# First convolution on TensorE in two row groups, start-up loads moved between queues, the last softmax inverse formed on VectorE, and a new order of both ends

## The chip, the cores and the metric

The kernel runs on one core of a Trainium2 chip. The core has TensorE (matrix products), VectorE, ScalarE and GpSimd (elementwise work), and SyncE, which here only issues transfers (DMA). The metric is device time in microseconds (us), lower is better. Names in profile rows: PE is TensorE, PEld its weight loads, DVE is VectorE, ACT is ScalarE, POOL is GpSimd, SP is SyncE; SPq and ACTq are the queues in which SyncE and ScalarE issue transfers.

## What is computed

The input is x of shape 4 x 128 x 64 x 64 (batch, channels, rows, columns). Layer 0 is a normalisation over channels, a depthwise 3x3 convolution with its input added, and attention of every pixel over its 5x5 neighbourhood inside a 16x16 window, in two branches of four heads. Layer 1 is a causal linear attention over the 4096 pixels of an image in order, then a recurrence over the pixels. Cut to what matters:

```python
y = layernorm2d(x, ln_g, ln_b)
y = y + cpe(y)                       # depthwise 3x3, edges repeated
q, k, v = Wq @ y, Wk @ y, Wv @ y     # per 16x16 window, branch and head
logits = q . patches(k) * scale      # 5x5 neighbours, zero outside the window
o = softmax(logits) . patches(v)
x = x + (Wo @ o, both branches) / rect
t = tokens(x)                        # 4 x 4096 x 128
t = t + num / den                    # elu features, cumulative sums of k v and of k
wx = batchnorm(layernorm(t) @ W.T)   # mean and variance over all tokens
y_t = sigmoid(wx_t + y_(t-1) @ V.T)  # along the 4096 tokens
out = t + y
```

A neighbour outside the window has a zero key, so it counts with a logit of 0: the denominator of the softmax is the sum over the neighbours inside plus the number of those outside, a constant of the pixel.

## The kernel before

**Tiling.** The image of a batch is cut into four bands of 16 rows (1,024 pixels), 16 bands in all, and a band into four windows of 16x16, 64 in all. Tiles have 128 channels or 128 pixels on the partitions.

**Steps of a band.** `norm_rows(n)` normalises the rows: `measured` takes statistics on VectorE (`bn_stats`, `bn_aggr`) and forms the inverse deviation on GpSimd with a power (L294, L295); `normed` scales on VectorE (L302); `turned` transposes on TensorE (L311); ScalarE evicts into `ypad`, a tile of 18 x 66 with its edges, which GpSimd fills by copies (L369 to L377). Then `taps` does the depthwise convolution: the first tap on ScalarE (L385), the other eight on VectorE (L387). The centre weight has 1 added, so that the input comes in with it (L820, on VectorE). For band 0 alone, two of four windows take another way, `multiply_first`: nine matmuls with diagonal matrices that ScalarE has made from the identity (L822), in two steps of four and five taps (L405). Windows 0 and 1 go through `convolve_first`, that is, `taps`.

**Steps of a window.** q, k (L436) and v (L449) are products with an eviction by ScalarE; v is moved between partition halves by two transfers (L458, L459). `logits` opens four PSUM banks with a mask product (L476), adds the products of q and k (L489), and ScalarE takes the exponentials (L498). `weighted` has three steps: sums (L518, with a copy `den` and a transfer that gathers it into a compact 128x32 tile `dc`, L526), values (L533, copy `o_sb` L541), and inverse: VectorE adds the count of outside neighbours (L544) and takes the reciprocal (L546), one transfer writes it to DRAM (`rd`, L550), another spreads it over all partitions (`rden`, L552). `scaled` multiplies `o_sb` by `rden` on GpSimd (L561) into `oT`, one tile for a band. `in_range` checks every four windows that the denominators are in range (L507, L508).

**Layer 1** works by half bands ("a" and "c"; in the end, "y" and "z" are those of the band before, "v" and "w" of the one before that): output projection and residual (L587, L594), measure, norm, turn, keys and queries (L634 to L638), values (L650), turn_keys (L663), scores (L671, L673), accumulate (L688, L696), attend (L707 to L721), keep (L726), measure_last, send and spread (per-token factors through DRAM, L618 and L629), and product (L748 to L755), which leaves the inputs of the recurrence. The last half, c of band 15, is normalised on the spot instead (norm_last, turn_last, L739 to L745).

**The recurrence** (L1026, L1031) runs over all segments at once after a global batch statistic (L741), with GpSimd adding and SyncE writing the output. It isn't touched.

**What sets the order.** Three lists of words. `START` is the order in which the first four windows are begun, with "front" as one step of the generator that prepares the following bands, and "warm.n" as n extra matmuls on zeros (`fill`, L268) before the next bank. `SLOT` with `AHEAD` and `LAYER1` is the order inside every later window. `TAIL` is the order of what remains after the logits of window 63. `in_order` (L912) then fixes that order on TensorE, VectorE, ScalarE and GpSimd; SyncE's queue isn't fixed by it. A weight tile comes in by `loaded`, on SyncE's or on ScalarE's queue:

```python
    load(0, 2)
    load_head(1)
    ln_g = loaded("ln_g", [P, 1], eng=nc.scalar)
    ln_b = loaded("ln_b", [P, 1], eng=nc.scalar)
    cpe_w = loaded("cpe_w", [P, 9], eng=nc.scalar)
    cpe_b = loaded("cpe_b", [P, 1], eng=nc.scalar)
    wqT = loaded("wqT", [P, BR * P], eng=nc.scalar)
```

## Time and profile before

| | us |
|---|---|
| median of 3 runs | 827.42 (825.77 to 827.80) |
| the profiled execution | 831.01 |
| its span | 829.3 |
| TensorE busy | 800.6 |
| VectorE busy | 689.7 |
| first q product starts (L436) | 19.37 |
| sums of window 3 (L518) start | 52.26 |
| first output projection (L587) starts | 67.31 |
| last logits (L489) end | 719.70 |
| output projection of the last band, half a (L587), starts | 734.40 |
| statistics of the last half (L740) end | 769.87 |

The times of the middle rows are from the start of the span, by the timeline and the chain of waits. The profile is of one execution; its own time is a little above the median of the others, so sums are made against it. In a row of the profile's groups the text reads: line, engine, operation, output <- input, partitions x elements, count, busy time, mean duration in ns of one, then the engine's idle time just before it and what ended that. A matmul with fp32 operands takes two passes, so TensorE shows twice the count of the source. A row of busy time by stretches reads: the stretch, its length, busy time (and count) of PE, PEld, DVE, ACT and POOL, the granted clock of TensorE as a share of full speed, the mean busy share of the 16 DMA engines, and GB/s.

### The profile page before, as it was taken

What the parts mean: (1) busy time and instruction counts of PE and PEld (TensorE: products, weight loads), DVE (VectorE), ACT (ScalarE), POOL (GpSimd) and SP (SyncE); (2) the same over time, 40 slices, a digit from 0 to 9 for tenths busy, and PEclk for the clock granted to TensorE, in tenths of its full rate; (3) what the DMA queues carried; (4) which work ended last, traced back from release to release, by engine and by line L of the source; (5) the groups of instructions that cost most, each with busy time, mean ns of one, the idle gap of its engine ahead of it and who ended that gap; (6) DMA issues with size and microseconds to landing.
All of it is one profiled execution on the core that took longest, in us unless ns stands there. A gap on an engine that the chain in (4) does not pass through costs nothing.

```text
span 829.3 us, 28925 instructions
## 1 busy us (share of the span) xinstructions
PE 800.6 (97%) x11811; PEld 642.3 (77%) x11817; DVE 689.7 (83%) x2134; ACT 530.6 (64%) x1022; POOL 254.9 (31%) x365
## 2 busy tenths in 40 slices
PE   7998999999999999999999999999999999988894
PEld 4776887878787878778787878788787878776693
DVE  6655989998989988998989898898989897378885
ACT  3775767676757576666767675766667675723683
POOL 2133241423233232413242322323231422231094
PEclk9998999999999999999999999999999999999997
DMA  5122141422323231414133232313141212211797
GB/s 142 21 64 71 43 120 39 88 75 69 85 70 96 62 100 33 114 42 112 48 84 77 63 93 70 96 39 108 43 120 41 80 53 69 69 53 39 240 206 206
DMA packets 81566, 69.33 MB, mean 84 GB/s; under 512 B 44816, under 2 KB 63888, under 8 KB 81424
## 3 DMA queue, kind: packets, MB, share of 16 engines
q1 hardware_dynamic: 53344, 44.00, 18.5%
q10 hardware_dynamic: 27072, 19.72, 8.8%
q0 software_dynamic: 1008, 3.67, 2.5%
q8 instruction: 95, 1.56, 0.9%
q14 instruction: 47, 0.39, 0.2%
HBM read 40.03 MB, written 17.89 MB: 70 GB/s over the span
## 4 chain that ended last, share of the span: by engine, by line
PE 89%; DVE 4%; DMA 3%; POOL 2%; issue 1%; ACT 0%; ACTq 0%; POOLq 0%; SPq 0%; DVEq 0%
PE bank L436 13%; PE bank L489 8%; PE bank L518 7%; PE bank L587 7%; PE bank L533 7%; PE bank L449 6%; PE bank L634 6%; PE bank L311 6%; PE z L1026 4%; PE bank L671 3%; PE bank L650 3%; PE bank L707 3%; PE bank L688 3%; PE bank L709 3%; PE bank L748 3%; PE bank L476 3%
## 5 line engine op out<-in xcount | busy, mean ns | idle before, releaser
L387 DVE SCALAR_TENSOR_TENSOR y<-ypad,cpe_w,y 128x512 f32<-128x512 f32 x240 | 184.2, 767 | 16.5 <-ACT y L385 12.0
L498 ACT ACTIVATE es<-bank 128x512 f32<-128x512 f32 x256 | 132.2, 602 | 32.4 <-PE bank L489 32.4
L294 POOL TENSOR_SCALAR rs<-mv 128x4 f32<-128x4 f32 (+2 forms) x100 | 25.5, 255 | 377.8 <-DVE mv L292 373.1
L561 POOL TENSOR_TENSOR oT<-o_sb,rden 128x512 f32<-128x512 f32 x64 | 83.4, 1304 | 122.1 <-DMA rden<-rd 87.4
L295 POOL TENSOR_TENSOR rs<-rs,mhalf 128x4 f32<-128x4 f32 (+2 forms) x100 | 106.0, 1060 | 8.3
L533 PEld LDWEIGHTS bank<-es,v_sb 128*32 128x32 f32 x3072 | 62.7, 110 | 37.0 <-issue 32.0
L444 ACT COPY k<-bank 128x512 f32<-128x512 f32 x64 | 38.6, 604 | 66.2 <-PE bank L436 66.2
L489 PE MATMUL bank<-q,k 32*64 32x160 f32 (+1 forms) x4096 | 77.6, 274 | 0.0
L489 PEld LDWEIGHTS bank<-q,k 32*64 32x64 f32 x4096 | 75.3, 130 | 2.7
L587 PEld LDWEIGHTS bank<-woT,oT 128*128 128x128 f32 x512 | 62.3, 199 | 12.7 <-POOL oT L561 8.9
L518 PE MATMUL bank<-es,ones 128*32 128x512 f32 x512 | 68.4, 605 | 0.1
L533 PE MATMUL bank<-es,v_sb 128*32 128x96 f32 (+1 forms) x3072 | 68.5, 237 | 0.0
L587 PE MATMUL bank<-woT,oT 128*128 128x128 f32 x512 | 63.2, 283 | 4.8 <-POOL oT L561 4.8
L436 PE MATMUL bank<-y2w,wqT 128*128 128x256 f32 x256 | 66.5, 382 | 0.7 <-DVE y2w L387 0.6
L521 ACT COPY den<-bank 128x512 f32<-128x512 f32 x64 | 37.4, 584 | 45.1 <-PE bank L518 45.0
L436 PE MATMUL bank<-y2w,wkT 128*128 128x256 f32 x256 | 66.0, 380 | 0.0
L449 PE MATMUL bank<-wvT,y2w 128*128 128x256 f32 x256 | 65.7, 379 | 0.0
L634 PE MATMUL bank<-xl,awT 128*128 128x512 f32 x128 | 63.1, 594 | 1.0 <-ACT xl L611 1.0
L636 ACT ACTIVATE low<-bank,minus 128x512 f32<-128x512 f32 x64 | 44.0, 687 | 21.9 <-PE bank L634 20.2
L544 DVE TENSOR_TENSOR dc<-dc,pad_c 128x32 f32<-128x32 f32 x64 | 23.7, 371 | 41.0 <-DMA dc<-den 40.8
L444 ACT COPY q<-bank 128x512 f32<-128x512 f32 x64 | 38.7, 605 | 27.6 <-PE bank L436 21.5
L290 DVE BATCH_NORM_STATS2 st<-x 128x6 f32<-128x128 f32 x256 | 55.3, 278 | 0.5
(137 smaller groups left out, 1685.8 us busy)
## 6 DMA issues: line engine op xcount, KB each, us to landing
rden<-rd SPq DMA_DIRECT2D x64, 256.0 KB
v_sb<-v_sb SPq DMA_DIRECT2D x128, 64.0 KB
factors<-factors ACTq DMA_DIRECT2D x31, 256.0 KB
xin<-in_xt SPq DMA_DIRECT2D x15, 512.0 KB
out<-rs_o ACTq DMA_DIRECT2D x16, 256.0 KB
resd<-rs_o ACTq DMA_DIRECT2D x16, 256.0 KB
out<-ot SPq DMA_DIRECT2D x32, 128.0 KB
out<-ys POOLq DMA_DIRECT2D x7, 512.0 KB, 7.3
```

The lines of the kernel that those rows point to most:

```text
L295: nc.gpsimd.tensor_tensor(rs[:, :n], rs[:, :n], mhalf[:, :n], ALU.pow)
L387: nc.vector.scalar_tensor_tensor(y2, src, cpe_w[:, tap : tap + 1], y2, ALU.mult, ALU.add)
L436: nc.tensor.matmul(pps[:, br * WT : (br + 1) * WT], wT[:, br * P : (br + 1) * P], y2, start=True, stop=True,)
L444: nc.scalar.copy(w[name], pps)
L449: nc.tensor.matmul(vps[:, e * 256 : (e + 1) * 256], y2[:, e * P : (e + 1) * P], wvT, start=True, stop=True,)
L489: nc.tensor.matmul(sps[h][half * KC : (half + 1) * KC, cols], w["k"][rows, k0 : k0 + KC], w["q"][rows, cols], start=False, stop=br == BR - ...
L498: nc.scalar.activation(es, sps[h], AF.Exp, scale=scale)
L518: nc.tensor.matmul(dps[rows], ones[:, :HD], w["es", h], start=True, stop=True)
L533: nc.tensor.matmul(ops[rows, cols], w["v"][:, n, c0 : c0 + HD], w["es", h][:, cols], start=(br, n) == pieces[0], stop=(br, n) == pieces[-1],)
L561: nc.gpsimd.tensor_tensor(oTs[n][:, :, :, wj * WS : (wj + 1) * WS], w["o"].rearrange("p (a r c) -> p a r c", a=BR, c=WS), w["rden"].rearra ...
L587: nc.tensor.matmul(yps[:, j * P : (j + 1) * P], oT[:, br, t], woT[:, br, :], start=br == 0, stop=br == BR - 1,)
L634: nc.tensor.matmul(zps, awT[:, m * P : (m + 1) * P], h.xl, start=True, stop=True)
```

## The change

It has four parts.

**Loads.** `cpe_w` is ScalarE's first transfer. The three weights of q, k and v, the two masks and `pad_c` are issued by SyncE, the weights ahead of the second band. A one-column exponential (`lead`) comes ahead of ScalarE's other work. The 1 is added to the centre weight on GpSimd.

**The first band.** `first_rows` replaces `norm_rows(0)`: it measures the first four pieces as one group, the other four and the head of the next band as a group of five, turns both, and fills the edges on GpSimd and VectorE. Window 0 is multiplied on TensorE in two row groups (`multiply_rows`, rows 0 to 6 and 7 to 15), window 2 as before, windows 1 and 3 by taps.

**The last softmax inverse.** For window 63 alone, `weighted` gets a constant `pad` with the counts of outside neighbours for all pixels, on all partitions. VectorE adds it to `den`, takes the reciprocal and multiplies `o_sb`, in two halves of eight rows, straight into `oT`; `scaled` isn't called for it. The step "inverse" is the first half, "rest" the second, "check" the range check on `dc`.

**The order.** `START` and `TAIL` are new. The extra matmuls of START go from 11 to 3, those of TAIL from 23 to 4.

```diff
 START = (
-    "prepare conv.0 front warm.3 mul.2 conv.1 mul.3 q.0",
-    "k.0 front front mul.2 v.0 q.1 k.1 front",
-    "logits.0 q.2 front front mul.3 front front v.1",
-    "sums.0 logits.1 front values.0 front front front k.2",
-    "inverse.0 scaled.0 v.2 front front load.2 front logits.2",
-    "front sums.1 front values.1 q.3 warm.6 sums.2 inverse.1",
-    "q.4 k.3 v.3 warm.2 front logits.3 scaled.1 front",
-    "values.2 inverse.2 front k.4 front v.4 front",
+    "warm.1 upper front front front conv.1 mul.2 lower",
+    "mul.2 conv.3 q.0 k.0 v.0 logits.0 q.1 front",
+    "sums.0 front q.2 values.0 front front k.1 v.1",
+    "prepare inverse.0 front front logits.1 scaled.0 k.2 front",
+    "q.3 sums.1 front v.2 k.3 front front logits.2",
+    "front values.1 inverse.1 front front front v.3 sums.2",
+    "q.4 load.2 values.2 front k.4 scaled.1 v.4 logits.3",
+    "front front inverse.2 warm.1 front warm.1 front",
 )
 TAIL = (
-    "output.y inverse.62 warm.1 output.z scaled.61 measure.z norm.z turn.z",
-    "values.z warm.2 sums.63 measure.y norm.y turn.y queries.y keys.y",
-    "warm.1 values.63 keep.w turn_keys.y send.w scores.y keys.z inverse.63",
-    "warm.4 scaled.62 values.y accumulate.y turn_keys.z spread.w scaled.63 attend0.y",
-    "queries.z attend1.y warm.1 measure_last.y send.y spread.y scores.z accumulate.z",
-    "output.a product.w keep.y measure.a attend0.z warm.2 output.c attend1.z",
-    "norm.a warm.2 measure_last.z product.v measure.c norm.c product.y keep.z",
-    "turn.a keys.a values.a turn.c queries.a keys.c queries.c warm.2",
-    "turn_keys.a scores.a accumulate.a send.z attend0.a attend1.a measure_last.a send.a",
-    "turn_keys.c warm.2 values.c scores.c accumulate.c attend0.c attend1.c spread.z",
-    "spread.a measure_last.c warm.2 warm.4 keep.a norm_last.c product.z turn_last.c",
-    "keep.c product.a product.c",
+    "output.y output.z measure.y norm.y turn.y scaled.61 warm.4 keys.y",
+    "inverse.62 measure.z send.w norm.z sums.63 values.63 values.y scaled.62",
+    "inverse.63 turn_keys.y keep.w turn.z rest.63 queries.y keys.z scores.y",
+    "queries.z values.z product.v output.a measure.a spread.w product.w accumulate.y",
+    "scores.z attend0.y attend1.y measure_last.y turn_keys.z accumulate.z attend0.z norm.a",
+    "attend1.z keep.y send.y output.c spread.y measure.c turn.a measure_last.z",
+    "norm.c keys.a values.a product.y queries.a turn.c turn_keys.a queries.c",
+    "keys.c keep.z scores.a scores.c accumulate.a send.z attend0.a spread.z",
+    "attend1.a check.63 values.c turn_keys.c measure_last.a send.a accumulate.c attend0.c",
+    "attend1.c measure_last.c norm_last.c keep.a product.z spread.a product.a keep.c",
+    "turn_last.c product.c",
 )
...
     load(0, 2)
     load_head(1)
+    cpe_w = loaded("cpe_w", [P, 9], eng=nc.scalar)
     ln_g = loaded("ln_g", [P, 1], eng=nc.scalar)
     ln_b = loaded("ln_b", [P, 1], eng=nc.scalar)
-    cpe_w = loaded("cpe_w", [P, 9], eng=nc.scalar)
     cpe_b = loaded("cpe_b", [P, 1], eng=nc.scalar)
-    wqT = loaded("wqT", [P, BR * P], eng=nc.scalar)
...
+    lead = const.tile([P, 1], F32, name="lead")
+    nc.scalar.activation(lead, ones[:, :1], AF.Exp)
+    wqT = loaded("wqT", [P, BR * P])
+    wkT = loaded("wkT", [P, BR * P])
+    wvT = loaded("wvT", [P, BR * P])
     load(1)
+    mask_k = loaded("mask_k", [P, P], BF16)
...
+    def first_rows():
...
+        upper = measured([xin[0][:, j, :] for j in range(4)], 1e-6)
+        lower = measured([xin[0][:, j, :] for j in range(4, 8)] + [heads.pop(1)], 1e-6)
+        xn = normed(upper, p2, "xf")
+        rows = turned(xn, 0, 4).rearrange("p (r w) -> p r w", w=W)
+        evict(y[:, 1:9, 1 : W + 1], rows)
+        edge(nc.gpsimd, y[:, 1:9, 0:1], y[:, 1:9, 1:2])
+        edge(nc.gpsimd, y[:, 0, : WS + 2], y[:, 1, : WS + 2])
...
+    def multiply_rows(r0, r1):
...
+        cps = bank()[:, : (r1 - r0) * WS]
+        for tap in range(9):
+            dy, dx = divmod(tap, 3)
+            src = ypads[0][:, r0 + dy : r1 + dy, dx : dx + WS]
+            nc.tensor.matmul(cps, diag[:, tap, :], src, start=tap == 0, stop=tap == 8)
+        nc.scalar.activation(
+            y2s[0, 0][:, 0, r0 * WS : r1 * WS], cps, AF.Identity, bias=cpe_b
+        )
...
+        if "pad" in w:
+            n, wj = places[w["at"]]
+            for half in range(2):
...
+                rden = view(w["pad"])
+                nc.vector.tensor_tensor(rden, view(den), rden, ALU.add)
+                nc.vector.reciprocal(rden, rden)
+                nc.vector.tensor_tensor(
+                    oTs[n][:, :, rs, wj * WS : (wj + 1) * WS], view(o_sb), rden, ALU.mult
+                )
+                yield
+            nc.vector.tensor_tensor(dc, dc, pad_c, ALU.add)
+            in_range(group)
+            yield
+            return
...
-    nc.vector.tensor_scalar(cpe_w[:, 4:5], cpe_w[:, 4:5], 1.0, None, ALU.add)
+    nc.gpsimd.tensor_scalar(cpe_w[:, 4:5], cpe_w[:, 4:5], 1.0, 1.0, ALU.add, ALU.mult)
...
-    run(norm_rows(0))
+    first_rows()
...
+    pad = p3.tile([P, NCH, P], F32, tag="xin", name="xin")
+    pad = pad.rearrange("p j t -> p (j t)")[:, : BR * WT]
+    nc.sync.dma_start(pad, ins["pad_q"].partition_broadcast(P))
+    windows[len(places) - 1]["pad"] = pad
```

## The prediction

> **What bounds the kernel now.** I read the page first, then the chain of waits over the first 80 us and the last 180 us, then busy time in stretches of about 2 us where the chain leaves TensorE.
>
> ```profile
> PE 800.6 (97%) x11811; PEld 642.3 (77%) x11817; DVE 689.7 (83%) x2134; ACT 530.6 (64%) x1022; POOL 254.9 (31%) x365
> PE 89%; DVE 4%; DMA 3%; POOL 2%; issue 1%; ACT 0%; ACTq 0%; POOLq 0%; SPq 0%; DVEq 0%
> ```
>
> TensorE is 89% of the chain. From window 4 to window 62 the instructions of TensorE and VectorE stand in the same order in both programs, so I look for a change in time only in the beginning (to the first output projection, L587, at 67.31 us), the end (719.7, the last logits, to 771.9, where the recurrence starts) and the loads. The chain of waits in the beginning (start, duration, what):
>
> ```profile
> 1.73 3.46 DMA cpe_w<-in_cpe_w
> ...
> 15.28 0.40 DVE y2w L387
> ...
> 19.37 1.99 PE bank L436 x8
> 21.36 2.23 PE bank L405 x10
> ...
> 29.80 2.22 PE bank L405 x10
> ...
> 55.46 3.93 DMA dc<-den
> ...
> 61.56 4.29 DMA rden<-rd
> 65.90 0.09 issue
> 65.99 1.27 POOL oT L561
> 67.26 0.04 issue
> 67.31 6.48 PE bank L587 x32
> ```
>
> Three things are seen. VectorE waits for a 4.5 KB load (cpe_w) before it measures anything. q.0 starts at 19.37, behind eight VectorE taps, and two more half convolutions (2.23 and 2.22 us) then lie on TensorE's path. From 55.46 to 67.31 window 3's softmax inverse goes through DRAM. TensorE runs out of work at 63.7, and then pays twice, as busy time in stretches shows:
>
> ```profile
> 64.00:66.00 2.00, 0.00 (x0) 0.00 (x0) 0.00 (x0) 1.68 (x4) 0.01 (x1) 1.00 0.56 165
> 66.00:68.00 2.00, 0.69 (x3) 0.70 (x4) 0.88 (x2) 0.56 (x1) 1.80 (x4) 0.51 0.01 1
> 69.70:71.40 1.70, 1.70 (x10) 1.70 (x10) 0.27 (x1) 0.00 (x0) 0.00 (x0) 0.50 0.25 55
> ```
>
> The column before the DMA share is the granted clock: 0.50 from 66 to 72.8, so that L587's 32 matmuls take 6.48 us instead of the 3.57 of their next band. The end has the same chain for window 63, but another limit behind it:
>
> ```profile
> 728.13 1.40 DMA rd<-rc
> 729.58 3.36 DMA rden<-rd
> 732.99 0.09 issue
> 733.08 1.27 POOL oT L561
> 734.40 2.05 PE bank L587 x16
> ...
> 769.27 0.61 DVE stats L740
> ```
>
> **Part 1, up to q.0.** cpe_w becomes ScalarE's first load and its addition moves to GpSimd. A slot of the DMA semaphores was free again at 3.85, when ScalarE issued wkT, and 0.5 MB had moved by 4.0 (180 to 304 GB/s from 2.0 on), so I take the first half band as landed at 3.9 (bounds 3.3 and 5.2) where VectorE began at 5.36. From there: four statistics and aggregations 1.07, GpSimd's pair 1.3, so scaling starts at 6.4. The five-column lower group is ready on GpSimd at about 8.0 (1.05 us for four columns, 0.56 for one, so some 1.25 for five), scaled by 9.5. TensorE turns it by 9.6. The early exponential on ScalarE takes its 1.28 us table load out of the way; the nine diagonals (2.74) end at 7.4 instead of 10.69, ahead of the first eviction. From 9.9 TensorE does upper (18 passes of 112 columns), four taps of window 2, lower (18 of 144), and five taps. A 256-column pass is 0.223 and a 128-column one 0.112, so 2.0+1.8+2.25+2.2 = 8.3, and q.0 is due at 18.2. Before: 19.37, gain 1.2. The early weight loads move to SyncE's queue, before xin of band 1, which therefore issues near 5.2 and not 4.03; it was there at 9.25 before, VectorE reads it at 11, so the cover is about 1 us. If it is short, VectorE queues conv.1 and conv.3 behind it (q.1 needs conv.1 at 22, it ends at 19).
>
> **Part 2, q.0 to sums.3.** Before this took 32.96 us (19.37 to 52.33), all TensorE. Out go the two half convolutions (4.45) and six fills net (eight down to two, 1.3); in comes prepare's two products (1.3). TensorE's rows sum to 27.1. But ScalarE has 25.5 us of copies and exponentials in the same stretch, and sums.0 to sums.3 stand close behind their logits: four exponentials take 2.06, covered by 1.3, 1.7, 1.7 and 0.4 of other TensorE work, so I add 0.4 to 1.6 at each, and 0.8 at q.4, whose taps VectorE ends near 40. sums.3 ends at 47.6; before it was 53.3. Gain so far 5.7.
>
> **Part 3, the first output.** The inverse of window 3 still goes through DRAM, so this stall is not removed. In the new SyncE queue its gathering stands behind rden of window 2, not behind two v copies (den was ready at 54.06 and went out at 55.46). den 48.3, landing 52, rc 52.6, rd 54.0, rden 58.2, GpSimd 59.5 to 60.4. TensorE's other work (9.8) ends at 57.6, so its gap shrinks from 3.6 to between 1.9 and 2.8, and the output starts 6.9 earlier. **The clock.** The row: after a gap of 3.6 us the clock was 0.50 for 6.8 us, which cost 2.9 at L587. The rule (Trainium skill, "TensorE: Matmul & The Clock Gate", section "What's actually happening"): half clock after an idle window of about 3.4 us, on a free-running grid. The cold stretches here (from 11.4, 66.0 and 772.6) fit multiples of 3.41, and a window with 1.7 us of matmuls (762.4 to 765.8) stayed warm. By the row's gap I would leave 2.9 in place; by the rule a gap of 2 to 3 pays nothing. I take the rule, less 1.3 for hand-offs I left out (0.05 to 0.2 each): the beginning gains 6.9+2.9-1.3 = **8.5**.
>
> **Part 4, the end.** Window 63's inverse loses the two transfers (4.8), GpSimd's 1.27 and their waits. VectorE instead adds, inverts and multiplies two halves of 128x256. The nearest rows:
>
> ```profile
> L718 DVE RECIPROCAL rd<-rd 128x2 f32<-128x2 f32 x8 | 1.3, 166 | 0.3
> L546 DVE RECIPROCAL rc<-dc 128x32 f32<-128x32 f32 x2 | 0.7, 352 | 0.1
> 719.70:769.90 50.20, 45.12 (x331) 34.20 (x335) 35.98 (x135) 15.48 (x26) 9.85 (x15) 1.00 0.17 49
> ```
>
> The two differ by 186 ns over 30 columns, 6.2 ns each, so 256 columns take 1.7. The skill ("VectorE: DVE Perf Modes", section "First, the fixed hardware budget") says that a reciprocal repeats its divide step 8 times; at its 0.96 GHz that would be an estimate of 8.3 ns, 2.2 us. The rows decide: 1.7, and with an addition and a product of 0.42 each, 2.5 a half, 5.1 in all; by the page 6.1. Output of a can then start at 727.3, when GpSimd has window 62, where it was 734.40. That 7 us does not come through: VectorE worked 35.98 us of 50.2 (last row, fourth figure; 38.5 with its hand-offs), and now carries 5.1 more, less 0.35 for rc. From 723.0 (den of 63) its queue is 42.5 us long, because steps of y and z that lay before 734 now stand behind the inverse. Waits in it: 1.4 for GpSimd's power ahead of the last normalisation (before it too: POOL L295 from 763.62, 1.02), about 2 for others. So stats of c end near 768.8, not 769.9: gain **1**, bounds -2 (waits of 5 us) to +5 (the old stage's waits were 11.7, if all were the transfer's). 19 of 23 fills go (0.22 each, 4.2); TensorE is not the bound here, so they are worth nothing unless the clock drops.
>
> Sundry: the constant for the last window (256 KB on SyncE) is issued near window 58 with a window to spare, 0. One more column in the statistics tiles, 0.
>
> **Sum.** The profiled execution took 831.01 around a span of 829.3; minus 8.5 and 1 it is 821.5. The runs have a median of 827.42, 3.6 below the profiled one, so 818 for the median.
>
> **The rivals.**
> *A, as above* (0.50): 814 to 822.
> *B, the stall at the first output keeps its length* (0.22): dc, rd and rden land no faster with the exponentials close by, or TensorE goes cold at the new gap. For it: the same three transfers, DMA share 0.56 in the stall. Against: they issue sooner. Only 4 to 5 remain of the beginning, none of the end: 823.
> *C, the end follows TensorE, not VectorE* (0.12): the 7 us at output a pass through, since VectorE waited 11.7 there. Against: its queue of 42.5. 8.5+6: 813.
> *D, slower: cold TensorE in the end* (0.10). The fills at 740 to 762 go, and with VectorE as the bound TensorE works in short bursts. Each cold window of 3.4 costs up to 1.7 of path; the end has 15 of them. It decides from six on (10 us, more than the 9.5 gained); ten give 835. For it: two windows after 63.7 did it. Against: some 40 us of matmuls in 50 leave few windows under 1.7.
> *E, the loads on one queue* (0.06): xin of band 1 and masks arrive 4 to 8 us late, VectorE's convs with it, and the gain before sums.3 is used up: 827.
>
> A measurement of this kernel tells 0.3%, 2.5 us, from no change. A, B and C are faster beyond that save for a part of B (0.83); E and that part are the same (0.07); D is slower (0.10). The range 812 to 825 takes A, most of B and C; reaching to E would add the bounds of little weight.
>
> **What would show it.** In the new profile: q.0's first L436 row near 18 (right: 17 to 20); the output of band 0 near 60; the clock near 1.0 in the two stretches after it; the output of a some 7 us nearer to the last logits, with VectorE nearly full behind it; the recurrence 51 us after the last logits instead of 52.2. Two reciprocals of 1.7 each. I am wrong if VectorE waits for xin of band 1 beyond 12 us, if the clock shows halves in the end, or if VectorE idles over 8 us there.

## The result, and the profile after

| | before | after |
|---|---|---|
| median, 6 runs each, same chip | 827.61 (825.77 to 829.74) | 824.20 (822.34 to 825.12) |
| ratio | | 0.9956 [0.9937, 0.9974] |
| a second time (e5) | 830.38 (36 runs) | 824.73 (18 runs) |
| ratio | | 0.9937 [0.9919, 0.9955] |
| the profiled execution | 831.01 | 824.40 |
| its span | 829.3 | 822.6 |

The change makes the kernel faster, by 3.4 us between the medians in the first comparison and by 5.7 in the second. The forecast was 9.4 (827.4 to 818): the sign is right and 824.2 lies within 812 to 825, but the gain is a third to three fifths of the forecast one.

The page of the kernel after still shows TensorE as the bound (busy time of the engines, then the chain's shares):

```profile
PE 795.0 (97%) x11808; PEld 638.0 (78%) x11808; DVE 694.0 (84%) x2141; ACT 530.2 (64%) x1024; POOL 252.4 (31%) x362
PE 87%; DVE 6%; DMA 3%; POOL 1%; ACT 1%; issue 1%; SPq 0%; ACTq 0%; DVEq 0%; POOLq 0%
```

TensorE works 5.6 us less (800.6 before) and its share of the chain falls by two points (89% before): the path has lost TensorE work, and the waits on it have not shrunk with it. The chain of waits in the beginning, of the kernel after (start, duration, what):

```profile
0.80 3.06 DMA xin<-in_xt
...
9.99 2.00 PE bank L452 x18
11.99 1.77 PE bank L440 x8
13.76 2.26 PE bank L452 x18
16.02 2.22 PE bank L440 x10
18.24 1.73 PE bank L483 x8
...
50.02 0.59 ACT den L568
50.61 0.02 issue
50.62 4.74 DMA dc<-den
...
56.00 1.41 DMA rd<-rc
...
57.55 3.88 DMA rden<-rd
...
61.56 1.27 POOL oT L628
...
62.88 3.84 PE bank L654 x32
```

The first load is now that of x and not cpe_w; the two row groups (L452) and window 2 (L440) lie end to end from 9.99, and q.0 starts at 18.08 (the chain's row for it begins at 18.24). Then the chain of window 3's inverse is there again, den to dc to rd to rden to GpSimd, and the first output projection starts at 62.88, 4.4 us earlier than before (67.31). By stretches (the columns as explained with the profile before; the granted clock stands ahead of the DMA share), the place of the old cold stretch:

```profile
60.00:62.00 2.00, 0.00 (x0) 0.00 (x0) 0.00 (x0) 2.00 (x5) 0.44 (x1) 1.00 0.50 142
62.00:64.00 2.00, 1.12 (x10) 1.12 (x11) 0.54 (x2) 0.95 (x2) 1.42 (x4) 1.00 0.05 8
64.00:66.00 2.00, 2.00 (x21) 2.00 (x20) 1.00 (x3) 0.00 (x0) 0.00 (x0) 1.00 0.06 8
```

TensorE still stands idle, 2.92 us, but the clock stayed at 1.00, and the output takes 3.67 us to the next q product where it took 6.32. The end, by the chain of waits:

```profile
716.63 3.46 DMA rden<-rd
...
720.23 1.27 POOL oT L628
...
721.54 2.07 PE bank L654 x16
...
761.22 0.61 DVE stats L807
```

Busy time from the last logits to the statistics of c, and then the row of the tile that holds window 63's inverse (durations in ns: smallest, median, largest):

```profile
712.10:761.80 49.70, 42.22 (x318) 32.07 (x316) 40.84 (x140) 15.21 (x26) 8.56 (x14) 1.00 0.17 44
```

```profile
L601 DVE RECIPROCAL xin<-xin x2: 1753/1753/1753, 716.3 to 719.0; 128x256 f32<-128x256 f32 x2
```

The output of a starts 9.4 us behind the last logits (712.12), where it started 14.7 behind them; it waits for window 62 on GpSimd now. VectorE is busy 40.84 of 49.70 us (fourth figure), where it was 35.98 of 50.20. The two reciprocals took 1.753 us each.

The two profiled executions differ by 6.7 us of span, and this is where:

| | forecast | the two traces |
|---|---|---|
| first output starts earlier (67.31, 62.88) | 6.9 | 4.4 |
| clock at the first output (6.32, 3.67), less 1.3 for hand-offs | 1.6 | 2.65 |
| first output to last logits | 0 | 0.5 |
| last logits to statistics of c (50.2, 49.7) | 1 | 0.5 |
| statistics of c to the end of the span (59.4, 60.8) | 0 | -1.4 |
| sum | 9.5 | 6.7 |

Two questions are open. Why did the first output come 2.5 us late? And why do the runs show 3.4 to 5.7 where the two traces show 6.7?

### The profile page after: what moved, and what is told of

Read it like the earlier page. It is cut to its first block, busy times and chain, and to the rows that moved or that the text cites. A ratio compares the mean times of both kernels' runs of the same rounds, so it can differ in the third digit from the quotient of the medians.

```text
span 822.6 us, 28912 instructions
## 1 busy us (share of the span) xinstructions
PE 795.0 (97%) x11808; PEld 638.0 (78%) x11808; DVE 694.0 (84%) x2141; ACT 530.2 (64%) x1024; POOL 252.4 (31%) x362
## 3 DMA queue, kind: packets, MB, share of 16 engines
q0 software_dynamic: 1008, 3.67, 2.6%
## 4 chain that ended last, share of the span: by engine, by line
PE 87%; DVE 6%; DMA 3%; POOL 1%; ACT 1%; issue 1%; SPq 0%; ACTq 0%; DVEq 0%; POOLq 0%
PE bank L483 13%; PE bank L536 7%; PE bank L565 7%; PE bank L654 7%; PE bank L701 7%; PE bank L496 6%; PE bank L580 6%; PE bank L313 5%; PE z L1102 5%; PE bank L717 3%; PE bank L738 3%; PE bank L815 3%; PE bank L755 3%; PE bank L774 3%; PE bank L776 3%; PE bank L523 3%
## 5 line engine op out<-in xcount | busy, mean ns | idle before, releaser
L421 DVE SCALAR_TENSOR_TENSOR y<-ypad,cpe_w,y 128x512 f32<-128x512 f32 x240 | 184.6, 769 | 12.1 <-ACT y L419 7.6
L628 POOL TENSOR_TENSOR oT<-o_sb,rden 128x512 f32<-128x512 f32 x63 | 81.3, 1290 | 114.5 <-DMA rden<-rd 85.6
L536 PE MATMUL bank<-q,k 32*64 32x96 f32 (+1 forms) x4096 | 77.5, 274 | 0.0
L565 PE MATMUL bank<-es,ones 128*32 128x512 f32 x512 | 71.2, 605 | 0.0
L654 PEld LDWEIGHTS bank<-woT,oT 128*128 128x128 f32 x512 | 59.5, 192 | 12.3 <-POOL oT L628 8.5
L654 PE MATMUL bank<-woT,oT 128*128 128x128 f32 x512 | 60.6, 276 | 4.5 <-POOL oT L628 4.5
L292 DVE BATCH_NORM_STATS2 st<-x 128x6 f32<-128x128 f32 x256 | 55.4, 279 | 0.6
L496 PEld LDWEIGHTS bank<-wvT,y2w 128*128 128x128 f32 x256 | 48.5, 190 | 7.5 <-DVE y L421 0.8
```

The lines of the kernel that those rows point to most:

```text
L292: nc.vector.bn_stats(st[:, j, :], piece)
L421: nc.vector.scalar_tensor_tensor(y2, src, cpe_w[:, tap : tap + 1], y2, ALU.mult, ALU.add)
L496: nc.tensor.matmul(vps[:, e * 256 : (e + 1) * 256], y2[:, e * P : (e + 1) * P], wvT, start=True, stop=True,)
L536: nc.tensor.matmul(sps[h][half * KC : (half + 1) * KC, cols], w["k"][rows, k0 : k0 + KC], w["q"][rows, cols], start=False, stop=br == BR - ...
L565: nc.tensor.matmul(dps[rows], ones[:, :HD], w["es", h], start=True, stop=True)
L628: nc.gpsimd.tensor_tensor(oTs[n][:, :, :, wj * WS : (wj + 1) * WS], w["o"].rearrange("p (a r c) -> p a r c", a=BR, c=WS), w["rden"].rearra ...
```

## Experiments

"Start" and "end" below are the two halves of the change. Each kernel was run beside the kernel before on the same chip, and the ratio is to it, with its 95% interval. Of each there is also one profiled execution; from it I give the start of the first output projection (out0), its length to the next product of q or k (3.57 to 3.68 at full clock) and the stretch at hand.

### What one execution is worth: the kernel before, once more (e1)

No edit.

> The kernel before once more, unchanged, for a second profile. Theory P (the profiled execution of before was a long one, most of the missing gain is in that): its span comes out 2 to 4 us under 829.3, and the trace shows where, at the first output projection (clock) or in the recurrence. Rival Q (the profile is typical and the kernel after loses in runs without a profile): the span is 829 again, with the clock at 0.5 from the first output on.

828.39 in 14 runs, ratio 0.9991 [0.9975, 1.0007]: the same kernel. Its profiled execution has a span of 827.0 where the first had 829.3. The first output, 6.32 long in the first profile, was 5.30 long here with nearly the same idle time ahead of it (3.60 and 3.50). So 1 of the 2.9 us that the forecast read from the profile as the price of the cold clock (half clock) belonged to that one execution: half clock lasted 6.83 us in the first trace (66.05 to 72.88) and 3.41 in this one (68.15 to 71.56).

### The two halves apart (e2, e12, e3)

e2 and e12 are one kernel, the start alone: TAIL as before, and in the end

```diff
-    pad = p3.tile([P, NCH, P], F32, tag="xin", name="xin")
...
-    windows[len(places) - 1]["pad"] = pad
```

e3 is the end alone: loads, START and `norm_rows(0)` as before, the new TAIL and `pad`.

> The change without its end: new loads, first rows and START, the old TAIL with window 63's inverse through DRAM. Theory (the beginning carries the gain): ratio 0.995 to 0.996, 3 to 4 us, and in the trace the last logits end near 712. Rival (the end gives part of it): ratio 0.998 or more.

> The changed kernel with the old TAIL and without the last window's inverse on VectorE (as e2), a second time. Asked: does the new end add anything to the new beginning? If the end is worth 1 us as forecast, this run comes out 1 us above the changed kernel (ratio to the kernel before 0.9945 to 0.995, where the changed kernel had 0.9937 and 0.9956); if the end adds nothing on top of the beginning, the ratio is 0.993 to 0.9945, as e2's 0.9932.

> The end alone: old loads and START, the last inverse on VectorE and the new TAIL. Theory (VectorE bounds the end, the 7 us at the output of a do not come through): ratio 0.998 to 1.001, and 51 to 52 us from the last logits to the recurrence. Rival (the fills that went cost clock, or the end gives several us): over 1.002, or under 0.997.

| | runs | median | ratio | out0, length |
|---|---|---|---|---|
| e2, start | 6 | 824.19 | 0.9932 [0.9907, 0.9957] | 63.05, 5.30 |
| e12, start | 15 | 825.08 | 0.9960 [0.9941, 0.9979] | 62.91, 5.30 |
| e3, end | 22 | 827.45 | 0.9979 [0.9966, 0.9993] | 66.03, 3.68 |

By the ratios the start alone is worth 3.3 (e12) and 5.6 us (e2), as much as the whole change (3.6 and 5.2): with it in place, nothing that the runs can tell from zero is left for the end. Alone, the end shows 1.7 us (0.6 to 2.8), but its one trace doesn't show them in the end: from the last logits to the statistics of c it is only 0.7 shorter (49.5 us against 50.2 to 50.5 with the old TAIL), and the first output, whose part of the program e3 leaves alone, came at least 0.9 earlier there than in the two traces of the kernel before, and at full clock. That one execution (824.11) was also the fastest of its 22. Where e3's 1.7 come from stays open.

The traces together say what the new end is worth. From the last logits to the statistics of c, the five with the old TAIL took 50.2, 50.5, 50.2, 50.3 and 50.2. Nine of the twelve with the new one (e11, which is another kind of run, left out) took 49.5 to 50.2, 49.9 on the mean, 0.4 less. The other three took 52.0 (e6), 52.5 (e10) and 52.3 (e16). The same stretch of the kernel after and of e10 (below) shows why, first the kernel after:

```profile
736.00:742.00 6.00, 5.52 (x25) 3.32 (x25) 5.05 (x17) 3.01 (x5) 2.40 (x4) 1.00 0.17 36
```

```profile
736.00:742.00 6.00, 5.38 (x16) 3.34 (x17) 3.74 (x16) 1.85 (x3) 2.40 (x4) 0.72 0.16 46
```

The same TensorE time holds 25 records there and 16 here, at a granted clock of 0.72. e6 shows 0.72 in this stretch too and e16 0.76; the nine others show 1.00. So rival D's mechanism, TensorE cold in an end with fewer extra matmuls, is real; it came in three of twelve executions, and these took some 2.4 us longer. (3.41 us at half clock can cost 1.7 of that at most; what the rest is was not looked into.) On the mean of the twelve the new end takes 50.5, 0.2 more than the old.

### The clock at the first output (e4, e5, e6)

e4 is the kernel before with 14 products on zeros in the gap, behind q.6:

```diff
+                if what == "q" and i == NB + 1:
+                    busy[0] += 14
```

e5 is the kernel after once more. e6 is the kernel after with 12 in the same place, and with 16 instead of 6 ahead of the recurrence:

```diff
+                if what == "q" and i == NB + 1:
+                    busy[0] += 12
...
-    fill(bank(), 6)
+    fill(bank(), 16)
```

> The kernel before with 14 matmuls on zeros (3.1 us) in TensorE's gap of 3.6 us ahead of the first output projection, so that it does not go idle there. If ordinary runs pay the half clock that the profile showed (2.9 us at that projection): ratio 0.9965, 2.5 to 3 us less. If that belongs to some executions only, depending on where the clock's window falls: half of that or less, 0.998 to 1.0.

> The kernel after once more, unchanged. Theory R (the recurrence and its writes vary by 1 to 2 us from run to run, and the first profile of after drew a long one): ratio 0.994 to 0.996, and from the statistics of c to the end about 59.5 us in this trace, not 60.8. Rival S (the new order lengthens the recurrence by 1 to 2 us each time): 60.5 or more again, with the ratio at 0.996.

> The kernel after with 12 matmuls on zeros in the gap ahead of the first output projection and 16 instead of 6 ahead of the recurrence, so that TensorE's clock has no idle window at either place. If half clock at these two places costs ordinary runs of after 1 to 3 us: ratio 0.001 to 0.003 under that of the kernel after run beside it, with the clock at 1.0 in both stretches. If the recurrence is held by its writes: only the first place counts, 0.001 or less.

e4: 827.32 in 22 runs, 0.9970 [0.9958, 0.9981]; the output takes 3.68 us, out0 67.61. So the cold clock costs the kernel before 1.6 to 3.5 us on the mean of its executions. e5: 824.73, out0 62.53. e6: 824.93 in 18 runs, 0.9933 [0.9916, 0.9950], out0 62.77, length 3.67: by the ratios 0.3 us better than e5, by the medians not, with intervals that overlap, so nothing is shown. The trace of e5, the same kernel as after, shows why the mean differs from one trace. Two stretches of 3.41 us of e5, then two of the kernel after:

```profile
59.46:62.87 3.41, 0.75 (x5) 0.34 (x5) 0.00 (x0) 2.79 (x7) 1.60 (x4) 1.00 0.28 67
62.87:66.28 3.41, 3.41 (x19) 3.41 (x18) 0.76 (x3) 0.62 (x1) 0.22 (x1) 0.50 0.03 5
```

```profile
61.02:64.44 3.42, 1.56 (x14) 1.56 (x15) 0.54 (x2) 1.93 (x4) 1.85 (x4) 1.00 0.17 35
64.44:67.85 3.41, 3.41 (x28) 3.26 (x26) 2.85 (x11) 0.23 (x1) 0.83 (x2) 1.00 0.20 76
```

In the kernel after, TensorE was idle for 2.92 us and stayed at full clock; in e5 it was idle for 2.66 and fell to half clock, and the output took 5.30. Here is idle time against length in every trace that has a gap of over 1 us, with TensorE's work in one stretch of 3.41 us ("work", explained below):

```
idle  work  length         idle  work  length         idle  work  length
3.75  0.28  6.62 (e9)      3.10  1.53  3.68 (e10)     2.61  1.10  5.30 (e14)
3.60  1.07  6.32 (before)  3.09  0.32  5.30 (e2)      2.40  1.63  3.68 (e3)
3.50  1.25  5.30 (e1)      2.92  1.56  3.67 (after)   2.31  1.15  5.27 (e13)
3.27  0.93  5.30 (e12)     2.66  0.75  5.30 (e5)      1.34  2.27  3.67 (e16)
```

The three gaps of 3.5 and more all cost something, 1.6 to 2.9 us. From 2.3 to 3.3 five of eight cost 1.6 and three nothing, and not the shorter ones. The position of the gap tells them apart. In every trace that has several, the starts of half clock lie whole multiples of 3.413 us from one another (in e13, 62.06 and 765.21 lie 206 of them apart), so they mark a grid of windows in that execution. "Work" is TensorE's busy time in the window of this grid that holds most of the gap: up to 1.25 us of it, and the next window is at half clock, eight times of eight; from 1.53 on it is at full clock, four times of four. The 2.31 of e13 lie almost wholly in one window, the 3.10 of e10 are divided over two (1.2 and 1.9). The two lengths over 6 have a second cold window behind the first.

The Trainium skill ("TensorE: Matmul & The Clock Gate", section "What's actually happening") says that the window is free-running, which fits: where a kernel's gap falls on the grid differs between two executions of it. It also says that half clock comes after an idle window of about 3.4 us; here a window with 1.25 us of matmuls was enough, and the measurement decides. The bound between 1.25 and 1.53 is that of this place only: elsewhere in these traces half clock followed windows with up to 2.3 us. In the end of the kernel, the three cold executions had 1.31 (e10), 1.45 (e6) and 1.48 us (e16) of matmuls in the window ahead of the cold one; over the 41 us behind the last logits the thinnest window of the nine others has 1.8, and that of the five with the old end 2.0.

### What held the first output: the exponentials or ScalarE's queue (e9, e10)

The rows of ScalarE in the kernel after, in order of time, around the copy of den.3 (start, duration, what, and the idle time before it with what ended it):

```profile
49.49 0.62 ACT L470 COPY y2w<-y 128x512 f32<-128x512 f32 x1 [0.81 <-DVE y L421]
50.02 0.58 ACT L568 COPY den<-bank 128x512 f32<-128x512 f32 x1
```

The copy of den stands behind one that waits for VectorE's taps of band 1. But the last exponential of window 3 ended at 48.68 in the same trace, and the last product of the sums, which needs it, runs from 49.19 to 49.78, so there are two suspects:

```profile
49.19 0.59 PE L565 MATMUL bank<-es,ones 128*32 128x512 f32 x1
```

e9 moves the logits of window 3 ahead:

```diff
-    "q.4 load.2 values.2 front k.4 scaled.1 v.4 logits.3",
+    "q.4 load.2 logits.3 front k.4 scaled.1 values.2 v.4",
```

e10 does that too, and moves the step with y2w behind the sums:

```diff
-    "front front inverse.2 warm.1 front warm.1 front",
+    "front front inverse.2 warm.1 front warm.1",
...
                 block(f"{what}.{i - 1}")
+                if what == "sums" and i == NB:
+                    next(ahead)
```

> The changed kernel with one line of START in another order: logits.3 (and so the four exponentials of window 3) stands ahead of k.4, values.2 and v.4. Asked: what held sums.3 and the copy of den.3 until 50.0 us, where the forecast had 47.6 to 48.3. Theory X, the exponentials (the fourth ended at 48.68): sums.3 ends near 48, den.3 is copied by 48.5, the first output starts 1.5 to 2 us earlier (near 61), and the time falls by about 1.5 us if TensorE is not cold there. Theory Y, ScalarE's queue: the copy of den.3 stands behind the copy of y2w of band 1, which waits until VectorE has ended its taps at 49.47; then sums.3 ends earlier but den.3 is still copied at about 50.0, the first output stays at 62.5 to 62.9, and the time does not change.

> As e9, and the last front step before the recurring order (it holds the last taps of band 1 and the copy of y2w behind them) stands behind sums.3, so that the copy of den.3 is no longer queued behind y2w on ScalarE. Theory Y: den.3 is copied near 48.3, the first output starts near 61, some 1.7 us earlier than in the changed kernel, and the time falls by 0 to 1.7. Theory X expects the same of it as of e9. If the first output still starts at 62.5 or later, the transfers took longer in turn and neither held it. The cost of the move: q.5 or its taps may come later by up to 0.6.

e9: 825.66 in 22 runs, 0.9965 [0.9949, 0.9981], out0 63.87. The sums of window 3 end at 48.23 in it, but the copy of den still starts at 49.92, behind y2w, and SyncE issues its gathering only at 52.65:

```profile
49.40 0.62 ACT L470 COPY y2w<-y 128x512 f32<-128x512 f32 x1 [1.92 <-DVE y L421]
49.92 0.58 ACT L568 COPY den<-bank 128x512 f32<-128x512 f32 x1
```

So taking the exponentials away (theory X) is not enough. It doesn't clear them: in the kernel after, the sums behind them end at 49.78, so both hold den to nearly the same moment. No run moved y2w alone.

e10 takes both away: 826.44 in 22 runs, 0.9972 [0.9956, 0.9988], out0 62.85. den comes early, but nothing comes of it. ScalarE, then SyncE's queue, in e10:

```profile
48.39 0.59 ACT L568 COPY den<-bank 128x512 f32<-128x512 f32 x1 [0.91 <-PE bank L565]
49.41 0.62 ACT L470 COPY y2w<-y 128x512 f32<-128x512 f32 x1 [0.43 <-DVE y L421]
```

```profile
49.55 0.62 SPq L619 DMA_DIRECT2D rden<-rd  x1
50.27 0.51 SPq L505 DMA_DIRECT2D v_sb<-v_sb  x1
50.83 0.59 SPq L506 DMA_DIRECT2D v_sb<-v_sb  x1
51.47 0.64 SPq L573 DMA_DIRECT2D dc<-den  x1
```

den.3 is there at 48.98, and its gathering (L573) goes out at 51.47, 0.85 later than in the kernel after (50.62): SyncE stands at rden of window 2 until rd has landed, and then has two copies of v to issue. In the kernel after these went out ahead of rd, at 46.04 and 46.56; the edit, which moves v.4 back, has put them behind it. That is the second thing in the way, and the edit has made it worse. Both runs are no better than the kernel after.

### SyncE's order and the one buffer of rden (e13, e14, e16)

e13 is the kernel after, with that one gathering issued by ScalarE:

```diff
-        nc.sync.dma_start(dc, den[:: HD // COPIES, :])
+        (nc.scalar if w["at"] == NB - 1 else nc.sync).dma_start(dc, den[:: HD // COPIES, :])
```

e14 is e10 with the same edit. e16 is e14 with a tile of its own for rden of window 3, in space that is not in use until the end:

```diff
+        if w["at"] == NB - 1:
+            rden = wx[:, B - 3].rearrange("p n s k -> p (n s k)")[:, : BR * WT]
+        else:
+            rden = p1.tile([P, BR * WT], F32, tag="rden", name="rden")
```

> The changed kernel, with the gathering of window 3's den issued from ScalarE's DMA queue right behind the copy of den, instead of from SyncE's queue. In the changed kernel den was copied at 50.60, SyncE's queue had passed rden of window 2 (issued 49.74) by 50.36, and the gathering, issued at 50.62, landed at 55.38 (4.7 us) behind the 256 KB of that rden. Theory Z, the transfer shares the 16 DMA engines with rden of window 2 whatever queue issues it: landing stays at 54 to 55.4 and the first output at 62.3 to 62.9. Theory Q, it waits behind those 256 KB in one queue: landing near 52.7, first output near 60.5.

> e10 (logits.3 early, the copy of y2w behind sums.3) with the gathering of den.3 issued from ScalarE's queue. In e10 den.3 was copied by 48.98, but SyncE's queue stood until 49.55 at rden of window 2, then issued two copies of v, and came to the gathering at 51.47; it landed at 55.43, no earlier than in the changed kernel. If SyncE's order is what held it: it is issued at 49.0, ahead of rden of window 2, lands at 51 to 52, and the first output starts at 59.5 to 60.5, 2.3 to 3.3 us earlier than e10's 62.85; the time then falls by 2 us against e10 unless TensorE is cold at the first output. If not, the first output stays at 62.5 or later.

> e14 with a buffer of its own for rden of window 3 (it has one buffer for all windows, so its loading for window 3 waits until GpSimd has multiplied window 2). In e14 rd of window 3 was issued at 52.51 and there by 53.9, but rden of window 3 only at 55.61, when GpSimd had ended window 2 at 55.59; it landed at 60.05. If that buffer is the last thing that holds it: rden is issued near 54.0, lands near 58.4, GpSimd ends near 59.8 and the first output starts at 59.8 to 60.4, which is the forecast's own value (60.4); the time falls by 0 to 1.5 us against e14, if it does not meet a cold window there. If the first output stays above 61, TensorE's own order or another wait holds it.

| | runs | median | ratio | out0, length |
|---|---|---|---|---|
| e13 | 11 | 825.72 | 0.9960 [0.9940, 0.9981] | 62.11, 5.27 |
| e14 | 6 | 821.08 | 0.9905 [0.9879, 0.9930] | 61.50, 5.30 |
| e16 | 6 | 821.81 | 0.9915 [0.9884, 0.9946] | 60.79, 3.67 |

In e13 the gathering landed at 53.23 (in 2.75 us) and not at 55.38, nearer to theory Q's 52.7 than to Z's 54 to 55.4, but that does not decide for Q: in e5, where SyncE issued it at 50.54 behind the same rden, it landed at 53.60, in 3.06. In the other traces with this beginning it took 4.7 (after, e2), 4.3 (e12) and 3.7 (e6), so one trace of e13 can't tell. And in both, little came of the earlier landing: out0 is 62.11 and 62.53. The rows of e13 for GpSimd and for VectorE say why:

```profile
53.18 1.27 POOL L628 TENSOR_TENSOR oT<-o_sb,rden 128x512 f32<-128x512 f32 x1
53.26 1.25 DVE L611 TENSOR_TENSOR dc<-dc,pad_c 128x32 f32<-128x32 f32 x1 [1.85 <-DMA dc<-den]
```

VectorE's addition of 128x32 takes 0.19 us in the kernel after, where it starts behind GpSimd's multiplication of window 2 (53.45 to 54.72). Here it starts within it and ends with it, at 54.51; in e5 it took 1.20, from 53.62 to 54.82, beside a multiplication from 53.50 to 54.78, and in e9 0.83, to 56.01, beside one that ended at 55.97. The Trainium skill ("SBUF — State Buffer", section "SBUF: two separate sides") has the rule for it: a VectorE operation with two inputs in SBUF and a GpSimd operation share a pair of ports, and whichever starts first keeps it for the whole instruction. The rows agree with it.

In e14 the gathering went out as soon as den was copied, and rd could be issued at 52.51. The chain of waits of e14 shows what is late next:

```profile
54.31 1.28 POOL oT L628
55.59 0.01 issue
55.61 4.44 DMA rden<-rd
...
60.18 1.28 POOL oT L628
61.46 0.04 issue
61.50 4.51 PE bank L654 x24
```

rden of window 3 waits until GpSimd has ended window 2, since rden has one buffer. e16 takes that wait away; its chain:

```profile
51.94 3.40 DMA rd<-rc
...
55.36 3.97 DMA wx<-rd
...
59.46 1.28 POOL oT L631
...
60.79 3.84 PE bank L657 x32
```

60.79, against 60.4 in the forecast and 62.88 in the kernel after. (rd took 3.40 in it, not the 1.41 of the other traces; what slowed it wasn't tried.) So of the 2.5 us that the forecast missed at this place, 2.1 are three waits that lie one behind the other: the late copy of den (exponentials and y2w), SyncE's order, and the one buffer of rden. Without the first alone nothing came earlier (e10), without the second alone 0.8 (e13), without the first two 1.4 (e14), without all three 2.1 (e16). These are single traces; the five that share the beginning of the kernel after (e2, e5, e6 and e12 besides it) lie between 62.53 and 63.05.

By their medians e14 and e16 are 6.8 us below the kernel before in the same runs, where the kernel after was 3.4 and 5.7 below it. e14's interval ends below that of the first comparison of the kernel after (0.9937) and overlaps that of the second (from 0.9919), so that they are faster than the change is likely, and not shown. e16 is not faster than e14 in the runs, though its first output comes 0.7 earlier.

### The inverse of window 3 without DRAM (e7, e8, e15, e11)

e7 does for window 3 what the change does for window 63:

```diff
+    pad3 = wx[:, B - 3].rearrange("p n s k -> p (n s k)")[:, : BR * WT]
+    nc.sync.dma_start(pad3, ins["pad_q"].partition_broadcast(P))
...
+                if i == 3:
+                    windows[i]["pad"] = pad3
...
+                if what == "inverse" and i == NB:
+                    block("rest.3")
```

(with the range check at the end of the same window). e8 is e7 with 16 products on zeros instead of 6 ahead of the recurrence. e11 was to be e7 with the edits of e10; but the step taken out of START was not put back behind the sums, so every later step of the preparing generator came one place late in the whole kernel. Its expectation speaks of what it was meant to be. e15 is that kernel as meant.

> The kernel after with window 3's softmax inverse on VectorE too, from a constant loaded at the start, so that the first output projection waits for no DRAM transfer. If the wait for dc, rd and rden sets that projection: it starts near 60 instead of 62.9, ratio 0.003 under that of after. If VectorE or ScalarE is late there in any case: 0.001 or less.

> As e7_inverse3, with 16 instead of 6 matmuls on zeros ahead of the recurrence. If half clock at the recurrence's start costs the whole kernel 1.7 us: ratio 0.001 to 0.002 under e7_inverse3. If the writes bound it: the same as e7_inverse3.

> As e10, with the inverse of window 3 on VectorE without DRAM as well (e7). In e7 VectorE's queue (taps of band 1 until 49.5, then statistics, then 5 us of inverse) set the first output at 60.55, not den.3. If VectorE bounds it, the first output stays within 0.5 us of e7 (60.1 to 61) and the time within 0.5 us of e7, about 823.3; if den.3 did, it comes near 59 and the time near 822.

> What e11 was meant to be: e10 with the inverse of window 3 on VectorE (e7). In e11 the front step that had been taken out of START was not put back behind sums.3, so that every later front step came one step late. Here it is put back. If VectorE bounds the first output in e7 (60.55), it stays at 60.1 to 61 and the time at about 0.993 of the kernel before, as e7; if den.3 did, the first output comes near 59 and the ratio is near 0.991. If this run is 50 us longer again, the late front step was not what e11 showed.

| | runs | median | ratio | out0, length |
|---|---|---|---|---|
| e7 | 7 | 823.25 | 0.9924 [0.9894, 0.9953] | 60.55, 3.57 |
| e8 | 6 | 823.31 | 0.9916 [0.9883, 0.9949] | 61.74, 3.57 |
| e15 | 6 | 822.96 | 0.9927 [0.9901, 0.9954] | 61.15, 3.57 |
| e11 | 6 | 881.01 | 1.0621 [1.0579, 1.0663] | |

With the DRAM way gone there is no gap and no cold clock at the output in any of the three. VectorE's 5 us of inverse then stand behind the statistics of band 2 and ahead of its scaling (56.6 to 59.5 in e7), so it lies on the path in e7 and e8, and in e15 a copy of v does (4.09 us from 51.42); out0 gains 1.1 to 2.3 and den.3's earlier copy (e15) adds nothing. (In e8 an addition that takes 0.34 us in e7's chain took 1.44 beside GpSimd's multiplication of window 2, so out0 comes 1.2 later than in e7.) The medians of e7 and e8 are about 1.5 below the kernel after in the same runs (e5), within the intervals.

e11 is a measurement that was not meant: the chain's shares and the costliest row of VectorE in it.

```profile
PE 49%; DVE 26%; DMA 10%; ACT 8%; issue 3%; POOL 3%; SPq 0%; DVEq 0%; ACTq 0%; POOLq 0%
L423 DVE SCALAR_TENSOR_TENSOR y<-ypad,cpe_w,y 128x512 f32<-128x512 f32 x240 | 183.7, 766 | 74.5 <-ACT y L421 70.5
```

This kernel takes 52 us more than the kernel before (881.01 against 828.66), and by the ratios some 57 more than e15, which does the same work with that one step in its place. VectorE's taps had 74.5 us of idle time ahead of them, 70.5 of it for the first tap on ScalarE (12.1 and 7.6 in the kernel after), and the copy of y2w that waits for the taps held den behind it (y2w 78.25, den 78.77 in one such place), as in the beginning of the kernel after, but in every band.

## Why the prediction was right or wrong

**Up to q.0: right.** Due at 18.2, came at 18.08. The first half band was taken as landed at 3.9; VectorE began at 3.88. The loads on one queue (rival E) didn't reach the path: VectorE read band 1 at 11.06 without a wait; it waited 1.98 us for the head of band 2 (to 14.74), and q.0 didn't move.

**sums.3 and den.3: the failed step.** "sums.3 ends at 47.6" and "den 48.3, landing 52": the sums ended at 49.78, den was copied by 50.60 and dc landed at 55.38. The 47.6 does not follow from its own terms. Exponentials of 2.06 us covered by 1.3, 1.7, 1.7 and 0.4 leave 0.76, 0.36, 0.36 and 1.66, with 0.8 for q.4 some 3.9; 18.2 + 27.1 + 3.9 is 49.2. So the wait for the exponentials was seen rightly and 1.6 us of it dropped in the adding. That sum alone is not what kept the output late: in e10, with den copied by 48.98, it came no earlier. The second half of the failed step is the path behind den. That ScalarE works in order and had y2w ahead of den was left out (e9). That SyncE works in order was named, for rden of window 2 ahead of the gathering, and given no time; in e10 SyncE could not pass that rden before 49.55 and then had v to issue.

**The first output, 6.9 earlier: mis-sized, 4.4.** Behind the two queues stands the one buffer of rden, which the forecast didn't look at (e14). With all three away it is 6.5 earlier (e16). The stall kept 2.92 us of idle TensorE, where the forecast had 1.9 to 2.8 and rival B the old 3.6. B came closest, in the time (823) and in what it left (4 to 5 us of the beginning, none of the end). Its first reason, transfers that land no faster, holds for dc (4.74 us, 3.93 before, 3.7 in the forecast) and not for rden (3.88, 4.29 before); its second, TensorE cold at the new gap, came in e5. It had nothing of the queues and the buffer.

**The clock: the rule as I used it failed.** "By the rule a gap of 2 to 3 pays nothing": of the eight gaps from 2.3 to 3.3, five paid 1.6. A window need not be idle to be followed by half clock; one with 1.25 us of matmuls was followed by it (e1), and the window that I quoted as warm with 1.7 has 1.99 in the trace. That the first trace of the kernel after paid nothing was luck, since e5, the same program, paid 1.6. And the 2.9 before were one execution's price; another paid 1.6 (e1). The fill is worth some 2.5 in the kernel before (e4) and some 0.3, if anything, in the kernel after (e6), so on the mean of executions the clock may give about 2; in the first pair of traces it gave 2.65. It is not where the gain was lost, but it is what lets two single traces differ by 3 us at this one place.

**The end: the place right, the 1 us mis-sized.** The reciprocals took 1.753 us, as the rows said (1.7), and not the 2.2 estimated from the Trainium skill ("VectorE: DVE Perf Modes", section "First, the fixed hardware budget"). VectorE bounds the end, and what came earlier at the output of a (5.3 of the 7 us) did not come through, so rival C is refuted. By busy time VectorE idled 8.9 us there (49.70 less 40.84), a little over the 8 that were to be a sign of being wrong; hand-offs of some 20 to 30 ns between its instructions are part of that. The gain is 0.5 in the first pair of traces and 0.4 in nine of twelve; in the other three, with rival D's mechanism, one cold window and not ten, more than that is lost again, and the times show nothing of the end on top of the start (e2, e12).

**From trace to median: wrong.** The forecast took 3.6 off, because the profiled execution before lay 3.6 above its median. After, the profiled execution (824.40) lies 0.2 above it. The difference is not an offset of profiling; it was that one execution's length, part of it the cold clock at 67 us, which the sum had taken as a saving too, and a low median: beside the later kernels the kernel before has medians of 827.83 to 830.38 in 11 to 52 runs, where the forecast had 827.42 from three. This alone is 3.4 of the 6.2 us between 818 and 824.2; the rest is the sum's own (821.5 forecast, 824.4 profiled), above all the 2.5 at the first output.

**Open.** From the statistics of c to the end, the two traces differ by 1.4 us to the other side. Over seventeen traces the recurrence (from its first product on) takes 53.3 with the old end (five, 52.3 to 54.8) and 53.4 with the new (twelve, 51.9 to 54.3): the spread is as wide as the effect, so I take it as one execution's, not as the change's. That is not shown: the second trace of the kernel after had 60.9 us from the statistics to the end where 59.5 was expected (e5), as rival S there had it, though with a ratio of 0.9937 and not S's 0.996, while the ten other traces with the new end had 56.9 to 59.9. What makes it spread was not tried. The stretch ahead of it, from the statistics to the first product, was 6.5 to 6.7 us or 5.0, in both kernels; in those of 6.6 and 6.7 a stretch of 3.41 us at half clock lies in it, in those of 5.0 none or the tail of one. 16 products on zeros instead of 6 there gave 6.5 in e6, where they began late, and 5.0 in e8.

## What to carry to other kernels

When a chain of transfers is to come earlier, look at what stands ahead of each of its steps in every in-order queue (the copy, the issue, the buffer, the port): taking one wait away shows little until the last is gone. Price an idle gap of TensorE over several executions, by how it lies across the clock's windows and not by its length alone, and don't take one profiled execution's distance from the median off a sum. Hand-written order counts for more than the work it orders: one preparing step late cost some 57 us, more than fifteen times what the change brought in its first comparison.

## What was not expected of the hardware

TensorE fell to half clock behind an idle gap of 2.31 us (e13) and not behind one of 3.10 (e10), in the same place of nearly the same program; what told them apart is the work left in one window of 3.41 us, 1.15 and 1.53 us. Two executions of one program took 3.67 and 5.30 us for the same 32 products. One program's gathering of 16 KB took 4.74 us in one execution and 3.06 in another (the kernel after and e5). And an addition of 0.19 us on VectorE took 1.25 where GpSimd was multiplying.
